# Head laid out anew with 20 quads of raw rows, and SyncE fetching the rows of every 54th quad by one DMA per edge

## The chip, the cores and the metric

One core of a Trainium2 chip runs the whole kernel. The metric is the device time of one execution, in microseconds (us). The engines are TensorE (PE, with its weight loads PEld), VectorE (DVE), ScalarE (ACT), GpSimd (POOL) and SyncE (SP); each works through its own queue of instructions in order and waits for the others by semaphores. DMAs are issued from SP, ACT and POOL and run beside the engines.

## The reference

A graph layer on 12500 nodes (64 scalars and 32 vectors of 3, D = 160 numbers each) and 400000 edges, which are sorted by destination. Cut to what matters:

```python
h_s = s @ lin1_ws * a / sqrt(64);  h_v = einsum('nci,cd->ndi', v, lin1_wv) * a / sqrt(32)
w = silu(edge_scalars @ fc_w1 / 8) @ fc_w2 / 8          # 224 weights for each edge, in five parts
es, ev = h_s[edge_src], h_v[edge_src]                   # a random row of 160 for each edge
m_s1 = w1 * es * e0;  m_v1 = w2 * es * e1;  m_v2 = w3 * ev * e0   # m_s2, m_v3: dot and cross products
agg = segment_sum(concat(m...), edge_dst)
out = layernorm(x + gated(sc(x) + agg @ lin2))
```

## The kernel before

**Edges.** 400000 edges are 3125 tiles of 128. Four tiles are a quad, and the main loop runs 784 steps of one quad (the last ones shorter). All engines' instructions are written out in the order of that loop (`manual_schedule`), so an engine's queue holds them as the code has them.

**Head.** Seven loads of nodes (`load`: xa, xz) are multiplied by lin1 and written as the table `h_tab` (12500 x 160) in DRAM. While the table is not there yet, GpSimd gathers rows of x itself ("raw rows") for 16 quads, every 30th from step 24 on, four gathers each (`gather_raw`), with indices loaded by `load_raw_columns` (raw_cols), and ACT writes them to `raw_tab`. Two raw quads follow each chunk of nodes, the rest the last chunk. `dt` (all destinations) is loaded by ACT at the end of the head; `rel`, the place of each edge in its window of 16 nodes, is made from it.

**A step.** `gather` issues four indirect DMAs on GpSimd (hg<-h_tab,idx, 128 rows of 640 B each; pool `deep`, four buffers). `weights` multiplies hid by w2 into PSUM (pw), `products` on VectorE multiplies pw by the gathered rows (pr), `select_quad` makes the one-hot matrix, and `add_tile` sums pr over a window of nodes (pa). Results are turned (pt), multiplied by lin2 (po, `second`) and added into acc; finished nodes leave through `finish`. In a raw quad the rows come back from `raw_tab` (rg), and six stages (`raw_stage`, one in each of the six steps before) turn them, multiply them by lin1 and find their factors, so that the step needs no gather.

**SyncE** issues the plain loads: idx and eat (indices and edge attributes, 15 steps at a time), es (edge scalars, two DMAs for 6 steps, two buffers), xs and xv (every 30 steps), rg, xt, and the stores of the output. Each DMA that is issued from SP or ACT signals one of eight semaphores in turn, and waits for the landing of the DMA that had the same one before.

Of the kernel before, what the change touches and what calls it, by code (L numbers as in the profile page):

```python
# [10 lines left out]
F32 = mybir.dt.float32  # L11
I32 = mybir.dt.int32
I16 = mybir.dt.int16
BF16 = mybir.dt.bfloat16
AF = mybir.ActivationFunctionType
OP = mybir.AluOpType
# [31 lines left out]
RAW_TILES = (0, 1, 3, 4)  # L48

CYC = [(i, (i + 1) % 3, (i + 2) % 3) for i in range(3)]  # L50
# [8 lines left out]
def gnn_kernel(  # L59
# [160 lines left out]

    def load_raw_columns(r):

        t = steps[RAW_STEPS[r]][2][0][0]
        assert [u for u, _, _ in steps[RAW_STEPS[r]][2]] == [t + k for k in RAW_TILES]
        k = 0
        while k < 5:
            g, u = divmod(t + k, GT)
            m = min(5 - k, GT - u)
            nc.sync.dma_start(raw_cols[:, r, k:k + m], src[g][:, u:u + m])
            k += m  # L230

# [12 lines left out]
    def load_bases():  # L244

        nc.sync.dma_start(row0, dst[0:1])
# [3 lines left out]
        nc.sync.dma_start(rows[:even], bounds[0, :even * NO].rearrange("(g k) -> g k", k=NO))  # L250
        if even < NG:
            nc.sync.dma_start(rows[even:, :NB - even * NO], bounds[:, even * NO:NB])
# [6 lines left out]
    with tc.tile_pool(name="nodes", bufs=len(starts)) as nodes, tc.tile_pool(  # L259
        name="nodes_ps", bufs=6, space=PSUM  # L260
    ) as nps, tc.tile_pool(name="z_ps", bufs=2, space=PSUM) as zps:
        loaded = []

        def load(c0):
# [15 lines left out]
        def load_maps():  # L280

            raw = ends_pool.tile([2 * S, NWT], F32, name="raw")
            for half in range(2):
                r = slice(half * S, (half + 1) * S)
                nc.sync.dma_start(w1[r, r], fc_w1)
                nc.sync.dma_start(raw[r], fc_w2)
            return raw
# [13 lines left out]

        load(starts[0])
        at = consts.tile([P, NT], F32, name="at")
        nc.scalar.dma_start(at, attr)
        ath = consts.tile([P, NT], F32, name="ath")
        nc.vector.tensor_scalar_mul(ath, at, 0.5)

        l1 = consts.tile([P, P], F32, name="l1")
        nc.vector.memset(l1, 0.0)
        nc.scalar.dma_start(l1[:S, :S], lin1_ws)  # L310
        for i in range(2):
            r = slice(S + i * V, S + (i + 1) * V)
            nc.scalar.dma_start(l1[r, r], lin1_wv)
        scales = [(l1[:S], 1.0 / math.sqrt(S)), (l1[S:], 1.0 / math.sqrt(V))]

        def scale():
            for m, by in scales:
                nc.vector.tensor_scalar_mul(m, m, by)
            scales.clear()

        def block_diagonal(name, w, n, scale, queue=nc.scalar):
            k = w.shape[0]
            m = consts.tile([n * k, n * k], F32, name=name)
            nc.vector.memset(m, 0.0)
            for i in range(n):
                queue.dma_start(m[i * k:(i + 1) * k, i * k:(i + 1) * k], w)
            if scale != 1.0:
                scales.append((m, scale))
            return m

        l1z = block_diagonal("l1z", lin1_wv, 4, 1.0 / math.sqrt(V))
        for m, by in scales:
            nc.scalar.mul(m, m, by)
        scales.clear()
        for i in range(3):
            nc.scalar.dma_start(l1v[i::3, i * V:(i + 1) * V], lin1_wv)
        scales.append((l1v, 1.0 / math.sqrt(V)))
        for r in range(4):
            load_raw_columns(r)
        for c0 in starts[1:3]:  # L340
            load(c0)
        for r in range(4, RAWS):
            load_raw_columns(r)
        load_bases()
# [10 lines left out]
        for k, c0 in enumerate(starts):  # L355
            if k + 3 < len(starts):
                load(starts[k + 3])
            elif k + 3 == len(starts):
                index(0)
            _, cn, quarters, cq, xa, xz = loaded[k]  # L360
            if c0 == 3 * CH:
                bases()
            ht = nodes.tile([P, 4 * U, D], F32, name="ht", bufs=3)
# [44 lines left out]
    raw = load_maps()  # L408
    load_chunk(0, nc.scalar)
    nc.scalar.dma_start(dt, dst)  # L410
    nc.vector.tensor_copy(iota_p, iota_i)
# [10 lines left out]
    nc.sync.dma_start(scs, sc_ws)  # L422
    scv = block_diagonal("scv", sc_wv, 3, 1.0 / math.sqrt(V), nc.sync)


# [11 lines left out]
    for to, part, pieces, w, r0, c0, by in maps:  # L437
        for k, piece in enumerate(pieces):
            four, at_p = divmod(PIECE[piece], 4)
            m = terms.setdefault((to, part, four), len(terms))  # L440
            at_r = at_p * V
            r = l2[at_r:at_r + V, m, c0:c0 + w.shape[1]]
            nc.sync.dma_start(r, w[r0 + k * V:r0 + (k + 1) * V])
            scales.append((r, by))
    assert len(terms) == 11
    scales.append((scs, 1.0 / math.sqrt(S)))

# [239 lines left out]
    with tc.tile_pool(  # L687
# [4 lines left out]
        name="deep", bufs=4  # L692
    ) as deep, tc.tile_pool(name="raw", bufs=1) as raw_pool, tc.tile_pool(name="pw_ps", bufs=2, space=PSUM) as pw_ps, tc.tile_pool(
        name="pa_ps", bufs=2, space=PSUM
# [24 lines left out]
        def fetch(n):  # L719
# [4 lines left out]
            if n + 6 < len(steps):  # L724
                c, i, _ = steps[n + 6]
                if i == 0:
                    load_chunk(c)

        turned_rows = {}
        attrs = {}  # L730

        def fetch_raw(n):

            if n + 8 in raw_of:
                T = n + 8
                rg = raw_pool.tile([P, Q, D], F32, name="rg", bufs=1)
                nc.sync.dma_start(rg.rearrange("p t d -> p (t d)"), raw_tab[raw_of[T]])
                attrs[T] = [rg]

        def raw_stage(T, k):  # L740
# [3 lines left out]
            def flat():  # L744
                return raw_pool.tile([P, Q * P], F32, name="flat", bufs=3)

# [43 lines left out]
            elif k in (2, 1):  # L790
                if k == 2:
                    turned_rows[T] = raw_pool.tile([P, Q, D], F32, name="hs", bufs=1)
                c = slice(0, S) if k == 2 else slice(S, D)
# [128 lines left out]
        with tc.manual_schedule(  # L922
# [9 lines left out]
            products_due = []  # L932
            checks = farthest(late)
            for n, (c, i, tiles) in enumerate(steps):
# [172 lines left out]
```

## Time and profile before

| | |
|---|---|
| median of 3 runs | 4002.86 us (4002.58 to 4004.17) |
| profiled execution | 4002.3 us, span 4000.5 us |
| TensorE busy | 3371.9 us (84%), granted clock 0.925 |
| VectorE busy | 2410.4 us (60%) |
| ScalarE busy | 1002.1 us (25%) |
| GpSimd busy | 2971.0 us (74%) |
| bytes moved | 422.84 MB, mean 106 GB/s |

Busy times are shares of the span. In a line of the groups stand line, engine, operation, out<-in and count, then busy time and mean ns of one, then the idle time of the engine before these instructions and what ended most of it. A line of the waits has the waiting engine and line, whom it waited for, and us in total, times and longest. In the order of time stand start, duration and instruction, with idle time before it in brackets; "x12" is a run of equal rows and its duration reaches from the first's start to the last's end. A line of windows has the length, then busy time of PE, PEld, DVE, ACT and POOL with counts, granted clock, busy share of the DMA engines and GB/s.

### The profile page before, as it was taken

How to read it: one execution, taken by the hardware profiler on the slowest of the kernel's cores; microseconds unless marked ns; L12 is line 12 of the kernel's file. 1: busy time of each engine (PE TensorE's matmuls, PEld its weight loads, DVE VectorE, ACT ScalarE, POOL GpSimd, SP SyncE). 2: the span in 40 equal slices, each digit the busy share in tenths (PEclk: the TensorE clock that was granted, in tenths of full speed). 3: DMA queues.
4: the chain of work that ended last, by engine and by line, in shares of the span. 5: the costliest groups of instructions: out<-in, count | busy, mean ns of one | idle time of the engine just before them, and what ended most of it. 6: DMA issues, size and time to landing. Idle time of an engine off the chain costs nothing. (4 is left out here: it accounts for less than half of the span.)

```text
span 4000.5 us, 55637 instructions
## 1 busy us (share of the span) xinstructions
PE 3371.9 (84%) x17991; PEld 1683.7 (42%) x17991; DVE 2410.4 (60%) x6505; ACT 1002.1 (25%) x3235; POOL 2971.0 (74%) x3133
## 2 busy tenths in 40 slices
PE   4598898898888889889899889788789888888887
PEld 4244444444444444444444444344344344344443
DVE  2465665666666666656666656556556565665655
ACT  0322222222222222223222222222122222221222
POOL 5677777777777777777777777777777777777775
PEclk7699999999999999999999999999899989999998
DMA  8634444434444443444444443444443443443442
GB/s 205 167 93 109 102 107 101 111 95 101 113 99 107 105 109 96 110 103 104 104 102 104 101 114 95 99 105 98 99 106 95 109 99 95 106 102 95 101 99 62
DMA packets 297291, 422.84 MB, mean 106 GB/s; under 512 B 76356, under 2 KB 241232, under 8 KB 296097
## 3 DMA queue, kind: packets, MB, share of 16 engines
q0 software_dynamic: 150000, 256.20, 24.9%
q1 hardware_dynamic: 130720, 147.26, 16.7%
q10 hardware_dynamic: 16274, 15.74, 1.3%
q8 instruction: 147, 2.41, 0.3%
q14 instruction: 150, 1.23, 0.1%
HBM read 397.71 MB, written 21.25 MB: 105 GB/s over the span
## 5 line engine op out<-in xcount | busy, mean ns | idle before, releaser
L490 POOL DMA_INDIRECT hg<-h_tab,idx x3061 | 2907.3, 950 | 946.9 <-issue 835.5
L578 PE MATMUL pa<-pr,sel 128*64 128x416 f32 x6250 | 1355.7, 557 | 1.4 <-DVE pw L557 1.4
L512 DVE TENSOR_TENSOR pr<-pw,hg 128x512 f32<-128x512 f32 x766 | 529.3, 691 | 1033.1 <-DMA hg<-h_tab,idx 1020.0
L502 PE MATMUL pw<-w,hid 64*128 64x224 f32 x6250 | 865.4, 392 | 338.3 <-DVE acc L611 227.0
L520 DVE TENSOR_TENSOR pr<-pw,hg 128x384 f32<-128x384 f32 x2298 | 1137.8, 547 | 0.0
L502 PEld LDWEIGHTS pw<-w,hid 64*128 64x128 f32 x6250 | 576.7, 195 | 635.6 <-issue 540.6
L578 PEld LDWEIGHTS pa<-pr,sel 128*64 128x64 f32 x6250 | 398.7, 143 | 576.5 <-issue 554.2
L850 ACT COPY sa<-pa 128x416 f32<-128x416 f32 x521 | 263.3, 505 | 1062.3 <-PE pa L578 1057.9
L481 PE MATMUL ph<-es,w 128*128 128x512 f32 (+1 forms) x784 | 455.5, 664 | 42.9 <-DMA es<-in_es_t_dram 29.8
L483 ACT ACTIVATE hid<-ph 128x512 f32<-128x512 f32 x392 | 233.6, 596 | 670.4 <-PE ph L481 670.0
L557 DVE TENSOR_TENSOR pw<-rel,iota_p 128x64 f32<-128x64 int16 x782 | 178.8, 229 | 339.6 <-PE pw L502 335.0
L587 PEld LDWEIGHTS pt<-ident,sa 128*128 128x128 f32 (+1 forms) x2084 | 223.8, 134 | 296.9 <-issue 231.1
L587 PE MATMUL pt<-ident,sa 128*128 128x128 f32 (+1 forms) x2084 | 337.0, 286 | 7.6 <-ACT hid L483 4.2
L603 PE MATMUL po<-tt,l 128*96 128x256 f32 (+3 forms) x1360 | 314.2, 378 | 13.8 <-DVE y L643 11.2
L571 DVE TENSOR_TENSOR sel<-pw,eas 128x256 f32<-128x256 f32 x766 | 317.2, 414 | 0.0
L591 ACT COPY tt<-pt 128x192 f32<-128x192 f32 x521 | 164.9, 316 | 487.8 <-PE pt L587 486.0
L603 PEld LDWEIGHTS po<-tt,l 128*96 128x96 f32 x1360 | 212.0, 164 | 124.5 <-issue 56.6
L481 PEld LDWEIGHTS ph<-es,w 128*128 128x128 f32 x784 | 121.8, 196 | 322.1 <-issue 230.8
L611 DVE TENSOR_TENSOR acc<-acc,os 96x32 f32 x1042 | 197.9, 190 | 24.0 <-ACT os L606 5.5
L637 PE MATMUL pp<-ident,acc 96*128 96x96 f32 x196 | 39.6, 288 | 94.4 <-DVE pw L557 45.8
L606 ACT COPY os<-po 96x512 f32<-96x512 f32 (+2 forms) x68 | 38.4, 564 | 317.4 <-PE po L603 301.9
L593 ACT COPY tt<-pt 128x32 f32<-128x32 f32 x521 | 102.2, 196 | 0.0
(105 smaller groups left out, 1123.6 us busy)
## 6 DMA issues: line engine op xcount, KB each, us to landing
es<-in_es_t_dram SPq DMA_DIRECT2D x258, 384.0 KB
hg<-h_tab,idx POOLq DMA_INDIRECT x3061
h_tab<-ht ACTq DMA_DIRECT2D x6, 1280.0 KB
xt<-in_x_dram SPq DMA_DIRECT2D x23, 320.0 KB
out_dram<-y SPq DMA_DIRECT2D x23, 320.0 KB
raw_tab<-raw_rows ACTq DMA_DIRECT2D x16, 320.0 KB
rg<-raw_tab SPq DMA_DIRECT2D x16, 320.0 KB
xv<-in_xv_t_dram SPq DMA_DIRECT2D x25, 187.5 KB
```

Source lines behind the costliest of these rows:

```text
L481: nc.tensor.matmul(ph[:k, c], w1[:k, :k], es[:k, t0 * P + c0 * P:t0 * P + c1 * P], start=True, stop=True)
L483: nc.scalar.activation(hid[:k, c], ph[:k, c], AF.Silu, scale=1.0 / math.sqrt(64))
L490: nc.gpsimd.indirect_dma_start(out=hg[:, t, :], out_offset=None, in_=h_tab, in_offset=bass.IndirectOffsetOnAxis(ap=i, axis=0))
L502: nc.tensor.matmul(pw[:, t, :NWT], hid[r, c * P:(c + 1) * P], w2[r], start=True, stop=True)
L512: nc.vector.tensor_mul(two, pw[:, :n, :2 * S].rearrange("p t (k c) -> p t k c", k=2), hg[:, :n, None, :S].to_broadcast([P, n, 2, S]))
L520: nc.vector.tensor_mul(pr[:, :n, first:first + V3].rearrange("p t (i c) -> p t i c", i=3), pw[:, :n, None, 2 * S + k * V:2 * S + (k + 1) * ...
L571: nc.vector.tensor_mul(sel[:, :n], oh[:, :, None, :].to_broadcast([P, n, 4, W]), e[:, :, :, None].to_broadcast([P, n, 4, W]))
L578: nc.tensor.matmul(pa[half * ROWS:(half + 1) * ROWS, :NPR], sel[:, t].rearrange("p k w -> p (k w)"), pr, start=start, stop=stop)
L587: nc.tensor.transpose(pt[:c, four * P:four * P + k], sa[:k, four * P:four * P + c], ident[:k, :k])
L603: nc.tensor.matmul(po[:, k, :nb], l2[:b, terms[to, part, four]], a[:, :nb], start=(n == 0), stop=(n == len(of) - 1))
L611: nc.vector.tensor_add(window, window, os[:, :, b])
L850: nc.scalar.copy(sa, pas.pop(j)[:, :NPR])
```

## The change

Three things are done. (1) The head has 20 raw quads instead of 16, three after each chunk of nodes; raw_cols comes in two DMAs ahead of everything else, all seven loads of nodes follow each other, and the first es and dt move from ACT's queue to SP's. The weights' diagonal blocks and the l2 matrix are loaded in fewer, wider DMAs and copied with a scale by VectorE. (2) Of 14 quads (steps 63, 117, ... 765) the rows are fetched by SyncE: four steps ahead of the start it loads the indices (cols), VectorE multiplies them by 640 and TensorE turns them, so that one partition holds 128 byte addresses (line). From step T - 51 on SyncE loads 32 of these at a time into registers and issues one DMA of 640 B for each edge, 512 for a quad, spread evenly over 49 steps. The one buffer hs takes the place of hg in step T. (3) Of the raw stages' buffers, flat has two instead of three, and rg and the result share one.

```diff
-RAWS = 16
+RAWS = 20
+OFF_FIRST = 63
+OFF_EVERY = 54
+OFF_LEAD = 51
+OFF_MARGIN = 2
+LOT = 32
 ...
+        load_raw_columns(0, 4)
+        nc.scalar.dma_start(l1[:S, :S], lin1_ws)
+        nc.scalar.dma_start(wv4, times(4, lin1_wv))
 ...
         load(starts[0])
+        load_raw_columns(4, RAWS)
+        for c0 in starts[1:]:
+            load(c0)
+        nc.sync.dma_start(row0, dst[0:1])
+        index(0)
+        raw = load_maps()
+        load_chunk(0)
+        nc.sync.dma_start(dt, dst)
 ...
-            rg = nodes.tile([P, Q, D], F32, name="raw_rows", bufs=8)
+            rg = nodes.tile([P, Q, D], F32, name="raw_rows", bufs=10)
 ...
-            for _ in range(2 if c0 < starts[-1] else len(raws)):
+            for _ in range(3 if c0 < starts[-1] else len(raws)):
                 gather_raw(raws.pop(0))
-    load_chunk(0, nc.scalar)
-    nc.scalar.dma_start(dt, dst)
 ...
+            def turn(self, cols):
+                nc.vector.tensor_scalar(at_byte, cols, float(ROW), None, op0=OP.mult)
+                nc.tensor.transpose(pl, at_byte, ident)
+                nc.vector.tensor_copy(line, pl)
 ...
+                def lot(k, p0):
+                    _, values = nc.values_load_multi_w_load_instructions(
+                        line[k:k + 1, p0:p0 + LOT], engines=[ENG.SP], min_val=0,
+                    for j, v in enumerate(values):
+                        nc.sync.dma_start(
+                            hs[p0 + j:p0 + j + 1, k].bitcast(U8),
+                            self.flat[ds(v, ROW)].rearrange("(o d) -> o d", o=1))
+                        yield
 ...
+                    if n == T - OFF_LEAD - 4:
+                        self.cols = self.begin(T)
+                    if n == T - OFF_LEAD - 1:
+                        self.line = self.turn(self.cols)
+                    if n == T - OFF_LEAD:
+                        self.todo.append((T, self.fetch(T, self.line), [0]))
 ...
+                    upto = min(Q * P, -(-Q * P * (n + 1 - T + OFF_LEAD) // of))
+                    while done[0] < upto:
+                        next(every)
+                        done[0] += 1
 ...
-                hg = (turned_rows.pop(n) if n in raw_of
+                off.step(n)
+                hg = (off.rows(n) if n in off.steps
+                      else turned_rows.pop(n) if n in raw_of
                       else gather(deep, [index(t) for t, _, _ in tiles]))
```

GpSimd's whole queue before, from the making of the identity on (raw_rows are gathers of x in the head, hg those of the main loop):

```order
masks.py:199 AFFINE_SELECT ident<-ident 128x128
L207 IOTA iota_i 128x128
L239 IOTA share 1x1042
L349 DMA raw_rows<-in_x_dram,raw_cols 128x160 x64
L490 DMA hg<-h_tab,idx 128x160 x3061
L1001 TENSOR_LOAD redo
```

and after:

```order
masks.py:199 AFFINE_SELECT ident<-ident 128x128
L216 IOTA iota_i 128x128
L248 IOTA share 1x1042
L351 DMA raw_rows<-in_x_dram,raw_cols 128x160 x80
L502 DMA hg<-h_tab,idx 128x160 x2989
L1098 TENSOR_LOAD redo
```

Sixteen gathers have moved into the head, and 56 are gone.

SyncE's queue before, at the first steps of the main loop:

```order
L159 DMA idx<-in_src_dram 128x60
L160 DMA eat<-in_ea_dram 128x240
L198 DMA es<-in_es_t_dram 64x4x384 x4
L824 DMA xs_1069<-in_xs_t_dram 64x500
L826 DMA xv_1071<-in_xv_t_dram 96x500
L737 DMA rg<-raw_tab 128x640
L159 DMA idx<-in_src_dram 128x5
L160 DMA eat<-in_ea_dram 128x20
```

and after, at the same place, where the first of the 14 quads begins:

```order
L168 DMA idx<-in_src_dram 128x60
L169 DMA eat<-in_ea_dram 128x240
L207 DMA es<-in_es_t_dram 64x4x384 x2
L760 DMA cols<-in_src_dram 128x2 x2
L207 DMA es<-in_es_t_dram 64x4x384 x2
L781 TENSOR_LOAD line
L786 DMA hs<-h_tab 1x640 x21
L917 DMA xs_1168<-in_xs_t_dram 64x500
L919 DMA xv_1170<-in_xv_t_dram 96x500
L786 DMA hs<-h_tab 1x640 x11
L781 TENSOR_LOAD line
L786 DMA hs<-h_tab 1x640 x10
```

Between the loads stand ten or eleven row DMAs for each step now, and every load is queued behind them.

ScalarE's queue before, at the end of the head (the last writes of the table, then what the main loop needs first):

```order
L400 DMA h_tab<-ht 128x160
L403 DMA h_tab<-ht 84x160
L352 DMA raw_tab<-raw_rows 128x640 x4
L198 DMA es<-in_es_t_dram 64x4x384 x2
L410 DMA dt<-in_dst_dram 128x3125
L483 ACT_TABLE_LOAD
```

and after:

```order
L399 DMA h_tab<-ht 128x160
L402 DMA h_tab<-ht 84x160
L354 DMA raw_tab<-raw_rows 128x640 x2
L408 DMA l1v<-in_lin_wv_dram 32x32 x3
L495 ACT_TABLE_LOAD
L495 ACTIVATE hid<-ph 128x512
```

es and dt have left it; they stand on SyncE behind the loads of nodes.

More of the change, by code (lines that the diff above doesn't have):

```diff
@@ L219, in gnn_kernel, with load_raw_columns @@
     nc.vector.memset(l1v, 0.0)
[L221 to L230, printed above, removed]
+    def load_raw_columns(a, b):
+        for r in range(a, b):
+            t = steps[RAW_STEPS[r]][2][0][0]
+            assert [u for u, _, _ in steps[RAW_STEPS[r]][2]] == [t + k for k in RAW_TILES]
+            assert divmod(t, GT) == (r, RAW_TILE0 - 5 * r) and t + 5 <= (r + 1) * GT
+        of = src[a][:, RAW_TILE0 - 5 * a:][:, :5]
+        nc.sync.dma_start(raw_cols[:, a:b],
+                          bass.AP(tensor=of.tensor, offset=of.offset,
+                                  ap=[of.ap[0], [P * GT - 5, b - a], [1, 5]]))
     w1 = consts.tile([2 * S, 2 * S], F32, name="w1")
@@ L262, in gnn_kernel, with times @@
         loaded = []
+        def times(n, w):
+            return bass.AP(tensor=w.tensor, offset=w.offset, ap=[[0, n], *w.ap])
         def load(c0):
@@ L285, in load_maps @@
                 nc.sync.dma_start(w1[r, r], fc_w1)
-                nc.sync.dma_start(raw[r], fc_w2)
+            nc.sync.dma_start(raw, times(2, fc_w2))
             return raw
@@ L305, in gnn_kernel @@
+        nc.scalar.dma_start(wv4, times(4, lin1_wv))
+        nc.vector.tensor_scalar_mul(l1[:S, :S], l1[:S, :S], 1.0 / math.sqrt(S))
+        for q in range(4):
+            r = slice(q * V, (q + 1) * V)
+            nc.vector.tensor_scalar_mul(l1z[r, r], wv4[r], 1.0 / math.sqrt(V))
+            if q >= 2:
+                nc.vector.tensor_scalar_mul(l1[r, r], wv4[r], 1.0 / math.sqrt(V))
         ath = consts.tile([P, NT], F32, name="ath")
         nc.vector.tensor_scalar_mul(ath, at, 0.5)
-        l1 = consts.tile([P, P], F32, name="l1")
@@ L309, in gnn_kernel @@
[L309 to L314, printed above, removed]
+        load(starts[0])
+        load_raw_columns(4, RAWS)
[5 more added lines that the diff above has]
+        load_chunk(0)
@@ L316, in scale @@
+        nc.sync.dma_start(dt, dst)
+        scales = []
         def scale():
-            for m, by in scales:
-                nc.vector.tensor_scalar_mul(m, m, by)
+            for m, of, by in scales:
+                nc.vector.tensor_scalar_mul(m, of, by)
             scales.clear()
[L321 to L344, printed above, removed]
@@ L355, in gnn_kernel @@
         for k, c0 in enumerate(starts):
[L356 to L359, printed above, removed]
             _, cn, quarters, cq, xa, xz = loaded[k]
             if c0 == 3 * CH:
+                load_bases()
                 bases()
@@ L403, in gnn_kernel @@
                 nc.scalar.dma_start(h_tab[c0 + full * P:c0 + cn, :], ht[:n, full])
-            for _ in range(2 if c0 < starts[-1] else len(raws)):
+            for _ in range(3 if c0 < starts[-1] else len(raws)):
                 gather_raw(raws.pop(0))
-    raw = load_maps()
-    load_chunk(0, nc.scalar)
-    nc.scalar.dma_start(dt, dst)
+    for i in range(3):
+        nc.scalar.dma_start(l1v[i::3, i * V:(i + 1) * V], lin1_wv)
+    scales.append((l1v, l1v, 1.0 / math.sqrt(V)))
     nc.vector.tensor_copy(iota_p, iota_i)
@@ L422, in gnn_kernel @@
     nc.sync.dma_start(scs, sc_ws)
-    scv = block_diagonal("scv", sc_wv, 3, 1.0 / math.sqrt(V), nc.sync)
+    scales.append((scs, scs, 1.0 / math.sqrt(S)))
+    scv = consts.tile([V3, V3], F32, name="scv")
+    nc.vector.memset(scv, 0.0)
+    wv3 = ends_pool.tile([V3, V], F32, name="wv3")
+    nc.sync.dma_start(wv3, bass.AP(tensor=sc_wv.tensor, offset=sc_wv.offset,
+                                   ap=[[0, 3], *sc_wv.ap]))
+    for i in range(3):
+        r = slice(i * V, (i + 1) * V)
+        scales.append((scv[r, r], wv3[r], 1.0 / math.sqrt(V)))
+    of_l2 = {}
+    for w, name in ((lin2_ws, "w2s"), (lin2_wv, "w2v")):
+        n = w.shape[0] // V
+        of_l2[name] = ends_pool.tile([P, n, w.shape[1]], F32, name=name)
+        for a in range(4):
+            nc.sync.dma_start(of_l2[name][a * V:(a + 1) * V],
+                              w.rearrange("(b r) c -> r b c", r=V))
     al_s = 0.25 / math.sqrt(96)
@@ L735, in fetch_raw @@
                 T = n + 8
[L736 removed]
+                rg = raw_pool.tile([P, Q, D], F32, name="rg", tag="rows", bufs=1)
                 nc.sync.dma_start(rg.rearrange("p t d -> p (t d)"), raw_tab[raw_of[T]])
@@ L933, in gnn_kernel @@
             checks = farthest(late)
+            off = Off()
+            assert not set(off.steps) & set(raw_of)
             for n, (c, i, tiles) in enumerate(steps):
```

65 lines of the change are left out of this document (57 added, 8 removed).

## The prediction

> **What bounds the kernel now.** I read the page's groups of instructions first, then the waits, then GpSimd's and VectorE's order of time at both ends.
>
> ```profile
> span 4000.5 us, 55637 instructions
> L490 POOL DMA_INDIRECT hg<-h_tab,idx x3061 | 2907.3, 950 | 946.9 <-issue 835.5
> DVE pr L512 <- DMA hg<-h_tab,idx: 1020.0, 431, 8.0
> POOL hg L490 <- DVE pr L520: 18.1, 44, 5.0
> 114.20 0.94 POOL L349 DMA_INDIRECT raw_rows<-in_x_dram,raw_cols  x1 [0.30 <-issue]
> 124.39 0.94 POOL L490 DMA_INDIRECT hg<-h_tab,idx  x1 [9.25 <-DMA l<-in_lin_wv_dram]
> 125.64 0.95 POOL L490 DMA_INDIRECT hg<-h_tab,idx  x1 [0.30 <-issue]
> 3968.39 0.94 POOL L490 DMA_INDIRECT hg<-h_tab,idx  x1 [0.30 <-DVE pw L557]
> ```
>
> GpSimd issues 3061 gathers between 124.39 and 3968.39 us: 3844.0 / 3060 = 1.256 us each, and the undisturbed pitch is 125.64 - 124.39 = 1.25. It is saturated: its own waits on VectorE are 18.1 us in all, while VectorE waits 1020 us for gathers. So the time is the head (124.4), 3061 pitches (3844), and 32.1 us from the last gather to the end of the span. The profiled execution took 4002.3 us against the median of 4002.86; I sum against 4002.3.
>
> TensorE is the next limit, and has room:
>
> ```profile
> 152.00:3970.00 3818.00, 3308.40 (x17639) 1631.48 (x17637) 2356.72 (x6356) 985.35 (x3194) 2889.77 (x3045) 0.94 0.42 102
> L786 PE MATMUL prt<-ident,rg 128*64 128x128 f32 (+1 forms) x128 | 19.9, 278 | 0.8 <-ACT hid L483 0.7
> ```
>
> The first number after the window's length is TensorE's busy time: 3308 / 784 steps = 4.22 us a step, VectorE's (third) 3.01. The granted clock is 0.94.
>
> **The change, part by part.**
>
> *Fewer gathers.* Four more raw quads and 14 quads for SyncE take 18 x 4 = 72 gathers out of the 3061: 72 x 1.256 = 90.4 us off GpSimd's steady part. The average step then has 2989 x 1.256 / 784 = 4.79 us. A raw quad issues 24 small matmuls, four quads 96 x 0.278 = 27 us on TensorE, and 14 transposes of offsets about 4 us: 4.26 us a step, 89% of 4.79. That lies beside the gathers, as long as the four buffers of hg even out the heavy steps. A skipped quad lets GpSimd run one step, 5 us, ahead; where a raw quad and a SyncE quad stand three steps apart (114 and 117, 171 and 174, 384 and 387) it may reach the end of its buffers. The longest such wait now is the 5.0 us above; I charge 8 us in all.
>
> *The head.* Sixteen more raw gathers stand in it, 16 x 1.25 = 20 us of GpSimd. Before, it starts them late and idles at the end:
>
> ```profile
> 14.18 1.10 POOL L349 DMA_INDIRECT raw_rows<-in_x_dram,raw_cols  x1 [11.73 <-DMA raw_cols<-in_src_dram]
> 17.36 23.61 SPq L229 DMA_DIRECT2D raw_cols<-in_src_dram  x12
> 0.00:50.00 50.00, 15.52 (x90) 15.06 (x91) 8.64 (x20) 2.21 (x4) 25.20 (x32) 0.73 0.63 130
> 50.00:100.00 50.00, 27.18 (x161) 25.01 (x160) 16.48 (x25) 1.15 (x3) 26.98 (x28) 0.75 0.98 280
> 100.00:150.00 50.00, 9.03 (x27) 4.26 (x25) 14.82 (x51) 6.11 (x11) 28.25 (x29) 0.53 0.77 227
> 123.81 0.77 ACTq L410 DMA_DIRECT2D dt<-in_dst_dram  x1
> 136.89 7.10 DVE L450 TENSOR_TENSOR rel<-dt,lo 128x520 int16<-128x520 int32 x6 [28.18 <-DMA dt<-in_dst_dram]
> 148.89 0.69 DVE L512 TENSOR_TENSOR pr<-pw,hg 128x512 f32<-128x512 f32 x1
> 151.25 0.94 POOL L490 DMA_INDIRECT hg<-h_tab,idx  x1 [5.03 <-DVE pr L520]
> ```
>
> Now the first index columns go out first on SyncE, so GpSimd starts near 5 us instead of 14.2, and 80 raw gathers end at 5 + 100 = 105 at the earliest. The other floor is the DMA engines: they move 280 GB/s when full (0.98 busy). Four more raw quads read and write 4 x 2 x 328 KB = 2.6 MB, and dt (1.6 MB) and the first es (0.8 MB) come ahead of the gathers instead of after: 5 MB more. By the windows 50 x 130 + 50 x 280 + 24.4 x 227 = 26 MB went before 124.4 us; 31 MB at 280 GB/s is 111 us, with a slow start 116. I take the first gather at 113 us (105 to 118): -11.4 us. dt now lands before the table is done, so rel stands off the path, the first product follows the first gather by some 6 us, and the 5.03 us wait at 151.25 goes: -5. What is late next there is the table itself, that is, the DMA engines.
>
> *SyncE's rows.* This decides. A quad is 512 DMAs of 640 B and 16 loads of 32 registers, all in SyncE's one queue, with a rotation of eight landing semaphores: each DMA waits for the one eight earlier. No DMA of one row at a register's address is in the trace; the nearest are those to or from one partition:
>
> ```profile
> 41.01 0.29 SPq L246 DMA_DIRECT2D row<-in_dst_dram  x1
> 45.33 0.30 SPq L250 DMA_DIRECT2D rows<-bounds  x1
> 45.68 0.25 SPq L252 DMA_DIRECT2D rows<-bounds  x1
> 45.98 0.49 SPq L270 DMA_DIRECT2D xa<-in_xs_t_dram  x1
> 2098.78 0.33 SPq L159 DMA_DIRECT2D idx<-in_src_dram  x1
> 2099.21 0.38 SPq L160 DMA_DIRECT2D eat<-in_ea_dram  x1
> 2099.69 35.49 SPq L198 DMA_DIRECT2D es<-in_es_t_dram  x4
> L875 DVEq TENSOR_LOAD <-rows x68: 543/1126/2425, 218.9 to 3980.5; - x68
> ```
>
> The pitch from one issue to the next is 45.98 - 45.68 = 0.30 for two elements of one partition, 0.35 (45.68 - 45.33) for 65 partitions, 0.43 (2099.21 - 2098.78) and 0.48 for 128. The far ends are 0.25 (the issue alone) and 23.61 / 12 = 1.97, where each issue waited behind the large loads. I take 0.30, the row nearest in shape: 512 x 0.30 = 154 us. A register load took 1.13 us for 16 values on VectorE and 0.54 at least, so some 0.04 a value, 1.8 us for 32: 16 x 1.8 = 29 us.
>
> [...]
>
> SyncE's other work and its present idleness come from its waits between 152 and 3970 us:
>
> ```profile
> SPq L198 <- PE pt L587: 1670.5, 83, 34.6
> SPq L159 <- DMA hg<-h_tab,idx: 883.5, 111, 28.9
> SPq L198 <- PE prt L786: 403.6, 14, 33.4
> SPq L675 <- DVE pw L557: 287.8, 20, 27.6
> SPq L198 <- PE ph L481: 209.9, 9, 32.9
> 122.31 1.39 ACTq L198 DMA_DIRECT2D es<-in_es_t_dram  x2
> 131.11 2.04 PE L481 MATMUL ph<-es,w 128*128 128x512 f32 x2 [29.79 <-DMA es<-in_es_t_dram]
> ```
>
> These five are 3455 of 3818 us, so its own loads take at most 363 / 14 = 26 us per 54 steps; I take 22, leaving the rest to waits too short to be listed here. New is that a row behind an es pair waits for its landing through the rotation: the pair landed 131.11 - 122.31 = 8.8 us after issue when the engines were full, and 3.1 us of that pass in issuing the pair and six rows. At 42% busy I take 6 us, a stall of 3, nine times in 54 steps, and 10 us for the other loads: 37 us (0 to 61). A quad is then 154 + 29 + 22 + 37 = 242 us.
>
> It may begin when VectorE has turned the columns at step T - 52, and must end by step T: 51.5 x 4.79 = 247 us. The next begins at T + 2, so the cycle is 242 + 3 steps = 256 us against 54 x 4.79 = 259. It fits, by 3 us. Once it doesn't, VectorE waits at step T, GpSimd fills its four buffers and stops, and every microsecond over costs 13 times itself.
>
> **Sum:** -90.4 - 11.4 - 5 + 8 = -98.8; 4002.3 - 98.8 = 3903.5 us, taken as 3904.
>
> **The rivals.**
>
> 1. *SyncE a little late.* Pitch 0.31 to 0.32, or 5 to 10 us more of stalls: cycle 260 to 266, 13 x (1 to 7) = 13 to 91 us given back: 3917 to 3995.
> 2. *SyncE is the bound: slower.* With a pitch of 0.35, as for 65 partitions, or a register's address costing 0.05 more: a quad 268, a cycle 280. SyncE's first quad begins at step 12, near 119 + 12 x 4.2 = 170 us; 170 + 268 + 13 x 280 + 19 x 4.79 + 31 = 4200 us. The point from which it decides: with a first quad of 255, (4000.5 - 170 - 255 - 122) / 13 = 266 us of cycle, a pitch of 0.32 (122 is the 19 steps and 31 us behind step 765). For it: the margin is 0.02 us an issue. Against it: the issue of two elements took 0.30 with its gap, and what a register's address adds no row shows.
> 3. *Each row costs what a load of 128 partitions does.* Pitch 0.43: a quad 308, a cycle 322: 170 + 308 + 13 x 322 + 122 = 4786 us. Against it: the single-partition rows are 0.25 to 0.30. [...]
> 4. *TensorE can't follow* a step of 4.79: half of the 90 us comes back, about 3950. Against it: 1020 us of VectorE waiting on gathers.
>
> **Chances.** Forecast 0.60 (3885 to 3925, from a first gather at 105 or 118 and 0 to 15 us of buffer waits). Rival 1 0.14, of which 0.05 lies within 0.2% (8 us, about what a measurement here can tell from none) and 0.01 beyond. Rival 2 0.14, rival 3 0.08, rival 4 0.04. So faster 0.60 + 0.08 + 0.04 = 0.72, same 0.05, slower 0.23. The range 3885 to 4100 leaves out most of rivals 2 and 3.
>
> **What would show it.** First gather near 113 us, first product some 6 us later; last gather 32 us before the end; a row's pitch on SyncE near 0.30 and SyncE still waiting for the turned offsets (line) or es buffers between quads. Wrong: VectorE waiting on DMAs of hs, with GpSimd waiting on VectorE just before; then the pitch or the stalls behind es were mis-sized. A gather's pitch above 1.26 would mean that 7168 small packets disturb the gathers.

## The result, and the profile after

The changed kernel takes 3930.36 us (median of 4 runs, 3926.78 to 3934.17) against 4002.84 for the kernel before, measured beside it: a ratio of 0.9821 with a 95% interval of 0.9806 to 0.9835. The forecast was 3904. The profiled execution took 3931.9 us for a span of 3929.8, 70.7 us shorter than the span before. The kernels below ran on several chips: on three of them, called slow chips here, the kernel before took 5196 to 5298 us at a granted clock near 0.83, on the others 4000 to 4003 us at 0.92 to 0.93, and each kernel is compared with before on its own chip.

GpSimd first: the page's groups, the waits, and GpSimd's order of time (start, length, engine, line) at the two ends of its gathers.

```profile
span 3929.8 us, 70593 instructions
L502 POOL DMA_INDIRECT hg<-h_tab,idx x2989 | 2837.5, 949 | 927.6 <-issue 800.8
DVE pr L524 <- DMA hg<-h_tab,idx: 836.4, 386, 5.7
POOL hg L502 <- DVE pr L532: 30.0, 77, 3.3
3.38 1.10 POOL L351 DMA_INDIRECT raw_rows<-in_x_dram,raw_cols  x1 [0.93 <-DMA raw_cols<-in_src_dram]
117.92 7.71 POOL L351 DMA_INDIRECT raw_rows<-in_x_dram,raw_cols  x1 [17.65 <-DMA raw_tab<-raw_rows]
128.44 0.95 POOL L351 DMA_INDIRECT raw_rows<-in_x_dram,raw_cols  x1 [0.30 <-issue]
139.28 0.94 POOL L502 DMA_INDIRECT hg<-h_tab,idx  x1 [9.90 <-DMA l1v<-in_lin_wv_dram]
3893.46 0.95 POOL L502 DMA_INDIRECT hg<-h_tab,idx  x1 [0.30 <-issue]
```

GpSimd still sets the pace: 2988 pitches between 139.28 and 3893.46 are 3754.2 us, 1.2564 us each against 1.2562 before, and VectorE still waits 836 us for gathers. The sum of the difference in span is then short:

| part | before | after | difference |
|---|---|---|---|
| 72 gathers fewer at 1.256 | | | -90.4 |
| first gather of the table | 124.39 | 139.28 | +14.9 |
| pitch over 2988 gathers | 1.2562 | 1.2564 | +0.6 |
| last gather to the end | 32.1 | 36.3 | +4.2 |
| all | 4000.5 | 3929.8 | -70.7 |

The gathers gave what they should; the head, which was to give 11.4 us, took 14.9. GpSimd itself stood in it: its last four raw gathers waited 17.65 us for a buffer that a write of raw rows still held, and ended at 129.4 us, not at 105. The first product follows the first gather by 6.7 us (145.99), where some 6 had been forecast.

Now SyncE: the tile view of the rows that it fetches (x count, nanoseconds min/median/max of one, first and last start in us), the same for its register loads, its waits, and a stretch of its order of time round one quad.

```profile
L786 SPq DMA_DIRECT2D hs<-h_tab x7168: 217/228/403, 202.0 to 3802.2; - x200
L786 SPq MOVE hs<-h_tab x7168: 29/29/38, 201.5 to 3802.2; - x200
  DVE pw L569: 0.8, 5
L781 SPq TENSOR_LOAD <-line x224: 1880/2130/2361, 199.0 to 3784.7; - x112
SPq L781 <- DVE pw L569: 164.1, 14, 16.2
SPq L786 <- DMA es<-in_es_t_dram: 152.4, 136, 2.5
1218.76 6.01 SPq L786 DMA_DIRECT2D hs<-h_tab  x10
1231.66 1.28 SPq L207 DMA_DIRECT2D es<-in_es_t_dram  x2
1240.97 23.08 SPq L786 DMA_DIRECT2D hs<-h_tab  x63
1469.49 6.24 SPq L786 DMA_DIRECT2D hs<-h_tab  x10
```

One quad runs from 1240.97 to 1475.7, 235 us. From the first row of the first quad to the last of the fourteenth are 3600.2 us; with a median of 237 us for a quad (by the issue times of all rows) the cycle is (3600.2 - 237) / 13 = 258.7 us, which is 54 steps of 4.79. The third row says whether it was enough: before the products that read hs, VectorE was idle 0.8 us behind its own work, and never for a DMA. SyncE instead waited for VectorE, at its first register load of each quad (164.1 us, 14 times).

### The profile page after: what moved, and what is told of

Same layout as the page of the kernel before. It is cut to its first block, busy times and chain, and to the rows that moved or that the text cites. A ratio compares the mean times of both kernels' runs of the same rounds, so it can differ in the third digit from the quotient of the medians.

```text
span 3929.8 us, 70593 instructions
## 1 busy us (share of the span) xinstructions
PE 3360.2 (86%) x18149; PEld 1685.3 (43%) x18149; DVE 2427.2 (62%) x6562; ACT 1011.0 (26%) x3252; POOL 2922.2 (74%) x3077
## 5 line engine op out<-in xcount | busy, mean ns | idle before, releaser
L502 POOL DMA_INDIRECT hg<-h_tab,idx x2989 | 2837.5, 949 | 927.6 <-issue 800.8
L590 PE MATMUL pa<-pr,sel 128*64 128x416 f32 x6250 | 1338.3, 551 | 1.4 <-DVE pw L569 1.4
L532 DVE TENSOR_TENSOR pr<-pw,hg 128x384 f32<-128x384 f32 x2244 | 1110.1, 547 | 0.0
L514 PE MATMUL pw<-w,hid 64*128 64x224 f32 x6250 | 847.6, 386 | 251.6 <-DVE acc L623 186.4
L524 DVE TENSOR_TENSOR pr<-pw,hg 128x512 f32<-128x512 f32 x748 | 516.9, 691 | 851.1 <-DMA hg<-h_tab,idx 836.4
L514 PEld LDWEIGHTS pw<-w,hid 64*128 64x128 f32 x6250 | 564.2, 192 | 543.3 <-issue 440.0
L351 POOL DMA_INDIRECT raw_rows<-in_x_dram,raw_cols x80 | 82.9, 1036 | 44.0 <-issue 22.2
```

Of the source, the lines that this page charges most:

```text
L502: nc.gpsimd.indirect_dma_start(out=hg[:, t, :], out_offset=None, in_=h_tab, in_offset=bass.IndirectOffsetOnAxis(ap=i, axis=0))
L514: nc.tensor.matmul(pw[:, t, :NWT], hid[r, c * P:(c + 1) * P], w2[r], start=True, stop=True)
L524: nc.vector.tensor_mul(two, pw[:, :n, :2 * S].rearrange("p t (k c) -> p t k c", k=2), hg[:, :n, None, :S].to_broadcast([P, n, 2, S]))
L532: nc.vector.tensor_mul(pr[:, :n, first:first + V3].rearrange("p t (i c) -> p t i c", i=3), pw[:, :n, None, 2 * S + k * V:2 * S + (k + 1) * ...
L590: nc.tensor.matmul(pa[half * ROWS:(half + 1) * ROWS, :NPR], sel[:, t].rearrange("p k w -> p (k w)"), pr, start=start, stop=stop)
```

## The experiments

Theory A of the study: the changed head is late, because its transfers stand one behind the other in two queues with one rotation of semaphores; the rest goes as forecast. Its rival, theory B: the head is bound by bytes. Beside that stands the question whether SyncE's rows have the narrow margin that the prediction gave them.

### The parts of the change, each alone

*e6_off_only*: the head of before with its 16 raw quads, and the 14 quads of SyncE. (It ran under the name e2_off_only on a slow chip as well, and the row-early kernel below as e1_row0_early; those are told at the end.)

```diff
+OFF_FIRST = 63
+OFF_EVERY = 54
+OFF_LEAD = 51
 ...
+            off = Off()
 ...
-                hg = (turned_rows.pop(n) if n in raw_of
+                off.step(n)
+                hg = (off.rows(n) if n in off.steps
```

(In part, and against the kernel before; the smaller buffers of the raw stages come along.)

> Head and 16 raw quads as before, the 14 quads on SyncE taken over, once more for a chip on which the gathers set the pace: 56 x 1.256 = 70 us less than before, 3932 us (3928 to 3940), first gather near 124 us, the gathers' pitch 1.256, no wait of VectorE for hs. Then the new head and the four more raw quads together bring nothing. If SyncE's rows disturb the gathers: pitch over 1.26, time over 3950.

3940.67 us, ratio 0.9848 [0.9832, 0.9865], 0.7 us above the range that was expected.

```profile
123.70 0.95 POOL L498 DMA_INDIRECT hg<-h_tab,idx  x1 [9.68 <-DMA l<-in_lin_wv_dram]
```

First gather 123.70, 3005 gathers at 1.2580, 36.1 us behind the last: 56 x 1.256 = 70.3 less for gathers, 5.4 more for the pitch, 4.0 more for the end. So SyncE's quads alone bring 61.7 us of span, and the new head with its four more raw quads, added to them, the other 9.0 of the change: not nothing, as the expectation had it.

*e9_no_off*: the new head with its 20 raw quads, no quad for SyncE.

```diff
-                self.steps = list(range(OFF_FIRST, len(steps) - 12, OFF_EVERY))
+                self.steps = []
```

> The changed kernel without any SyncE quad (their list of steps is empty; the head with 20 raw quads stays): 3045 gathers. Theory A (the time is first gather + gathers x 1.2564 + about 32 to 36, and the head of the change gives the first gather at 139 instead of 124): 139 + 3044 x 1.2564 + 32 = 3996 and 2 us around the span, 3998: within 0.3% of before, so 16 gathers fewer bought nothing. Theory B (the head itself gives the 20 us of its 16 gathers, and it is the SyncE quads that delay the start): first gather near 124, time about 3982.

3986.94 us, ratio 0.9967 [0.9955, 0.9978].

```profile
135.48 0.94 POOL L502 DMA_INDIRECT hg<-h_tab,idx  x1 [9.20 <-DMA l1v<-in_lin_wv_dram]
POOL hg L502 <- DVE pr L532: 10.7, 35, 0.3
```

It has theory A's late start (135.48, 11 us behind before), but a better time than its 3998. The pitch is 1.2539, 0.0023 x 3044 = 7.0 us less than before: the wait of 5.03 us at 151.25 is gone, as the prediction said, and little else waits: the 10.7 us of waits for VectorE's products are 35 ordinary pauses of 0.30. So 16 gathers fewer (-20.1), the head (+11.1), the pitch (-7.0) and the rest (+0.3) are -15.7, against the measured -15.9 of span. With SyncE's quads the pitch goes back to 1.2564, 0.0025 x 2988 = 7.5 us: those are the waits for buffers that were charged at 8. The waits show them: 30.0 us in 77 in the change are 77 pauses of 0.30 and 6.9 us more. The smaller buffers of the raw stages are in this kernel too, and cost nothing that its sum shows.

### SyncE's margin

*e8_every48*: a quad every 48 steps instead of 54, all else as changed.

```diff
-OFF_EVERY = 54
-OFF_LEAD = 51
+OFF_EVERY = 48
+OFF_LEAD = 45
```

> The changed kernel with a SyncE quad every 48 steps (lead 45) instead of 54 (51): 16 quads instead of 14, so 8 gathers, 10 us of GpSimd, fewer; SyncE needs about 237 us a quad and some 13 to 18 between two, 250 to 255, against 48 x 4.8 = 230 us of a cycle. Theory A (SyncE's own issue sets a hard limit just under the spacing of 54 steps): SyncE binds, each cycle is about 250 us instead of 230, VectorE waits for hs or for what stands on SyncE behind the rows, and the time is 4150 to 4300. Theory B (the rows are not near a limit, the cycle that was seen was only paced by the gathers): 3918 to 3930.

4234.3 us, ratio 1.0583 [1.0561, 1.0604]. It makes 15 quads, not the 16 that I had counted. The tile view of hs, the group of the first product that reads it, and VectorE's wait:

```profile
L786 SPq DMA_DIRECT2D hs<-h_tab x7680: 217/227/399, 229.2 to 3982.0; - x197
  DVE pr L524: 210.5, 14
L524 DVE TENSOR_TENSOR pr<-pw,hs 128x512 f32<-128x512 f32 x15 | 10.4, 692 | 223.4 <-DMA hs<-h_tab 210.5
L493 PE MATMUL ph<-es,w 128*128 128x512 f32 (+1 forms) x784 | 503.9, 728 | 496.6 <-DMA es<-in_es_t_dram 486.5
```

Now SyncE binds. A row costs what it cost before (227 ns). The cycle is (3982.0 - 229.2 - 240) / 14 = 250.9 us, where 48 steps would be 229.9: 14 x 21.0 = 294 us lost, against 304 between the medians of this kernel and of the change. VectorE waits 210 us for hs, and TensorE 487 us for es, which stands in the same queue behind the rows. So SyncE needs 250.9 us from quad to quad here; the change allows 258.7. The margin is 8 us in 259, and six steps closer costs the whole gain four times over.

### The head

The windows of the head in before and in the changed kernel, in four stretches up to the first gather of the table (the columns are busy time and count of PE, PEld, DVE, ACT and POOL; the last three are the granted clock, the busy share of the DMA engines, and GB/s):

```profile
0.00:30.00 30.00, 10.27 (x56) 9.81 (x56) 1.90 (x9) 2.21 (x4) 12.38 (x19) 0.84 0.74 144
30.00:70.00 40.00, 16.26 (x102) 14.91 (x102) 15.99 (x24) 0.00 (x0) 27.96 (x29) 0.67 0.77 208
70.00:100.00 30.00, 16.16 (x91) 15.36 (x92) 7.23 (x11) 1.15 (x3) 11.84 (x13) 0.73 0.91 261
100.00:124.40 24.40, 1.32 (x7) 0.89 (x5) 2.02 (x13) 0.00 (x0) 11.50 (x14) 0.50 0.88 278
```

```profile
0.00:30.00 30.00, 10.16 (x73) 9.97 (x73) 9.40 (x25) 0.00 (x0) 20.89 (x28) 1.00 0.95 173
30.00:70.00 40.00, 9.28 (x48) 8.63 (x48) 4.15 (x6) 0.71 (x1) 30.25 (x32) 0.59 0.99 281
70.00:100.00 30.00, 5.41 (x13) 3.31 (x14) 4.05 (x5) 1.82 (x4) 22.77 (x24) 0.50 0.77 189
100.00:139.30 39.30, 15.65 (x125) 14.59 (x124) 19.41 (x41) 0.72 (x1) 10.84 (x6) 0.72 0.90 284
```

The whole head, up to the first gather of the table, as rows of before, the change, e5 and e7 (told below), and the bytes moved in the first two:

```profile
0.00:124.40 124.40, 44.02 (x254) 40.97 (x254) 27.14 (x57) 3.36 (x7) 63.68 (x73) 0.69 0.82 219
0.00:139.30 139.30, 40.49 (x256) 36.49 (x256) 37.01 (x77) 3.25 (x5) 84.75 (x89) 0.69 0.91 238
0.00:132.40 132.40, 48.30 (x256) 43.22 (x256) 36.76 (x75) 3.02 (x5) 78.70 (x88) 0.72 0.93 246
0.00:130.50 130.50, 45.99 (x256) 41.49 (x256) 36.87 (x75) 3.12 (x5) 78.42 (x88) 0.70 0.92 250
```

```profile
DMA packets 24856, 27.26 MB, mean 219 GB/s; under 512 B 6248, under 2 KB 20241, under 8 KB 24082
DMA packets 27788, 33.22 MB, mean 238 GB/s; under 512 B 6929, under 2 KB 22277, under 8 KB 26886
```

The change has 6.0 MB more to move before its first gather. Two of its stretches are slow. In the first 30 us the DMA engines are 0.95 busy and still move only 173 GB/s. Between 70 and 100 there is a hole, 0.77 busy and 189 GB/s, in which TensorE and VectorE stand idle. This is what stood in it (order of time of SyncE, VectorE and TensorE, and SyncE's wait):

```profile
85.19 0.31 SPq L336 DMA_DIRECT2D row<-in_dst_dram  x1
92.89 0.83 DVE L255 COPY bases_row<-row 1x1042 int32<-1x1042 int32 x1 [49.35 <-DMA row<-in_dst_dram]
94.59 3.99 PE L308 MATMUL hp<-base_f,ones 1*128 1x512 f32 x6 [51.79 <-DVE base_f L304]
SPq L283 <- DMA h_tab<-ht: 43.1, 3, 16.5
```

The row of destinations, 12 KB, is queued on SyncE behind the loads of all seven chunks of nodes; those wait in the rotation of semaphores for writes of the table, 43.1 us in three waits; and the copy of that row, and the matmuls on it, stand on VectorE and TensorE ahead of the fourth chunk. A load issued at 85.19 (at 41.01 before) therefore holds four of seven chunks until 98.6.

*e5_row0_early*: this one load moved forward.

```diff
         load(starts[0])
+        nc.sync.dma_start(row0, dst[0:1])
         load_raw_columns(4, RAWS)
         for c0 in starts[1:]:
             load(c0)
-        nc.sync.dma_start(row0, dst[0:1])
```

> The kernel with row loaded behind the first chunk's loads once more, for a chip on which TensorE's granted clock is near 0.93 and the gathers set the pace, as in the two profiles compared. Theory A (VectorE, TensorE and ScalarE stand still for row from 42.8 to 92.9 us, and that delays the table): VectorE's wait for row falls under 10 us and the first gather comes at 118 to 130 us instead of 139.3, the time at 3908 to 3922 us. Rival B (the DMA engines or the rotation of semaphores set the head): the wait goes, the first gather stays at 135 to 140, the time within 4 us of 3930.

3923.71 us, ratio 0.9802 [0.9785, 0.9818]. VectorE no longer waits for the row, and the hole is full:

```profile
0.00:30.00 30.00, 10.90 (x73) 10.71 (x73) 9.20 (x25) 0.00 (x0) 21.82 (x29) 1.00 0.93 173
70.00:100.00 30.00, 15.75 (x88) 15.35 (x88) 8.06 (x17) 2.44 (x4) 22.67 (x24) 0.72 0.94 269
```

But the first gather came only 6.9 us earlier, at 132.42, outside what theory A had given and outside rival B's 135 to 140 as well; so was the time. The size of this gain is less sure than one trace makes it: the head of the changed kernel, line for line the same, gave its first gather at 139.28 in the change, 137.04 in e8 and 135.48 in e9, so the row is worth 3 to 7 us, and the intervals of the two ratios overlap. So the hole was one cause, and not the whole. GpSimd's wait for a buffer has gone with it: the raw gathers end at 107.3 us here, and GpSimd then waits 25.2 us for the first gather of the table.

*e7_raw_writes_later*: in addition the writes of raw rows issued on ScalarE's queue one chunk later, behind the next write of the table.

```diff
-            nc.scalar.dma_start(raw_tab[r], rg.rearrange("p t d -> p (t d)"))
+            held.append((r, rg))
 ...
+            write_raw(len(held))
             for _ in range(3 if c0 < starts[-1] else len(raws)):
                 gather_raw(raws.pop(0))
+        write_raw(len(held))
```

> The changed kernel with the row of destinations loaded early (as in e5_row0_early) and, beside it, each chunk's three writes of raw rows issued on ScalarE's queue behind the next chunk's write of the table, not ahead of it. Theory A (what the first gather still waits for in e5 is ScalarE's queue, in which the table's writes stand behind writes of raw rows that wait for their gathers and for the rotation of semaphores): the table's last write goes out near 105 us instead of 123.18, the first gather of the table at 110 to 120 instead of 132.42 (not ahead of the last raw gather, 106.33 in e5), and the time falls by the same 12 to 22 us, to 3902 to 3912. Theory B (the first 120 us are bound by the bytes of all DMAs, so their order on one queue only moves the wait): the first gather stays at 128 to 134, time 3920 to 3926.

3920.61 us, ratio 0.9798 [0.9781, 0.9814], first gather at 130.52. Its interval overlaps e5's; it is the fastest kernel of the study by the median. Theory B's numbers came true, but this run doesn't show its cause. These are the last writes on ScalarE's queue and the first gather behind them, in the change and then in e7:

```profile
132.61 0.86 ACTq L402 DMA_DIRECT2D h_tab<-ht  x1
133.66 1.03 ACTq L354 DMA_DIRECT2D raw_tab<-raw_rows  x2
118.15 0.56 ACTq L408 DMA_DIRECT2D h_tab<-ht  x1
121.94 4.71 ACTq L358 DMA_DIRECT2D raw_tab<-raw_rows  x5
130.52 0.95 POOL L510 DMA_INDIRECT hg<-h_tab,idx  x1 [16.19 <-DMA l1v<-in_lin_wv_dram]
```

The first gather follows the issue of the last raw rows by 3.9 us in e7 and 4.6 in the change, but that of the table's last write by 11.8 and 5.8. The semaphores in the traces say why: ahead of its first gather GpSimd's queue waits in turn for all eight semaphores of the loads and writes (from 134.3 to 138.6 us in the change), so for the writes of raw rows too. In the change the table had landed at 136.9 us and the last raw rows at 138.5, and the gather started 0.8 us later; in e7 the table had landed by 125.1, the raw rows at 129.7, and again the gather started 0.8 us later. (The view puts both waits down to l1v, whose loads use the same semaphores.) The raw rows lie in the pool of the head (`nodes`), which ends where the buffers of the main loop begin; that this is why the gather has to wait for them no run shows by itself. So e7 put later what the first gather waits for, and what the table's writes alone would have given it can't tell.

Up to the first gather the DMA engines' busy time is 0.82 x 124.4 = 102 us in before, 0.91 x 139.3 = 127 in the change, 0.93 x 132.4 = 123 in e5 and 0.92 x 130.5 = 120 in e7. So the change raised the busy time by 25 us, which speaks for the bytes; but e5 and e7, which move the same rows in another order, took 4 to 7 us of it back, so busy time isn't a floor that the order leaves alone. How much of the late start is bytes and how much order stays open.

### The runs on slow chips

*e12_quarter_writes* was to test theory B by itself: as many transfers, in the same order, with fewer bytes.

```diff
-            nc.scalar.dma_start(raw_tab[r], rg.rearrange("p t d -> p (t d)"))
+            nc.scalar.dma_start(raw_tab[r][:, :D], rg[:, 0, :])
 ...
-                nc.sync.dma_start(rg.rearrange("p t d -> p (t d)"), raw_tab[raw_of[T]])
+                nc.sync.dma_start(rg, raw_tab[raw_of[T]][:, None, :D].to_broadcast([P, Q, D]))
```

> The changed kernel, in which each of the 20 writes of raw rows carries a quarter of its bytes (the first of the quad's four tiles, which is later read four times over; the other three tiles' rows are left out of the output). The number of transfers, their order, their queues and their waits are the same; 4.9 MB of the head's 33 MB are gone. Theory B (the start is bound by the bytes of all transfers, 239 GB/s over the first 139 us): the first gather comes 4.9 MB / 0.239 = 20 us earlier, 119 instead of 139.3, and the time is 20 us less, about 3911. Theory A (the start is a chain of waits between SyncE's and ScalarE's queues, which the size of the transfers only lengthens): the first gather stays at 131 to 140, time 3923 to 3932. Should the chip be the one on which before takes 5200 to 5300 us, the first gather stands against 157 there: 137 by B, over 149 by A.

5557.89 us, where before takes 5297.63 (1.0495 [1.0457, 1.0534]). First gather at 161.78, against 157 for this head on such chips (157.3 in e11 and 157.1 in e3, on two other slow chips): 4.9 MB fewer and no gain, as theory A says. There the engines are not full:

```profile
30.00:70.00 40.00, 7.49 (x20) 5.91 (x21) 2.03 (x3) 0.00 (x0) 28.88 (x31) 0.50 0.56 139
SPq L287 <- DMA h_tab<-ht: 50.9, 1, 50.9
```

One wait of SyncE for a write of the table, through the rotation, lasts 50.9 us there. So on that chip fewer bytes didn't help; it doesn't tell what they would bring where the engines are 0.91 busy. That stays untested.

*e10_raw_writes_last*: the row early, and 18 of the 20 writes of raw rows behind the whole table, with two buffers fewer for the nodes.

```diff
-            rg = nodes.tile([P, Q, D], F32, name="raw_rows", bufs=10)
+            rg = nodes.tile([P, Q, D], F32, name="raw_rows", bufs=RAWS - 2)
 ...
+            if c0 in starts[:2]:
+                load(starts[-2 + c0 // CH])
 ...
+        write_raw(len(held))
```

> The changed kernel with the row of destinations early, and 18 of the 20 writes of raw rows (5.9 MB) issued on ScalarE only behind the last write of the table and the loads of l1v; for their 18 buffers the node loads have 5 instead of 7, so the last two chunks are loaded as the first two are done. Theory B of the last run (the first gather waits for bytes: 33 MB at about 240 GB/s, a share of 0.91 of the DMA engines over the first 139 us of the changed kernel): 5.9 MB fewer ahead of the table are 20 to 24 us, the first gather of the table comes at 108 to 118 instead of 130.5 (the raw gathers alone end near 106), and the time is 3899 to 3910. Theory A (something other than the bytes, the chain of loads, chunks and writes with its rotation of semaphores, holds the table): the first gather stays at 126 to 134, time 3917 to 3926. If the writes that are now late hold a buffer that a first gather of the table needs, the first gather is early and the second or third quad waits for it, and up to 20 us come back.

5475.45 us against 5196.22 (1.0564 [1.049, 1.0639]). The first gather is later, not earlier:

```profile
173.30 0.94 POOL L513 DMA_INDIRECT hg<-h_tab,idx  x1 [50.42 <-issue]
146.43 21.20 ACTq L354 DMA_DIRECT2D raw_tab<-raw_rows  x18
SPq L287 <- DMA raw_tab<-raw_rows: 33.9, 1, 33.9
```

Two things meet: a load of nodes on SyncE waits 33.9 us, through the rotation, for a write of raw rows that stands on ScalarE; and GpSimd's first gather starts only as the 18 late writes end. The view names no releaser for the second, but it fits the wait that the semaphores of the change and of e7 show: the last raw rows went out at 167.6, and the gather came 5.7 us later, with the table long written. The expectation had allowed for buffers only of the second or third quad. Neither theory is decided by it.

*e11_no_last_quad* was to explain the 4 us longer end.

```diff
-                self.steps = list(range(OFF_FIRST, len(steps) - 12, OFF_EVERY))
+                self.steps = list(range(OFF_FIRST, len(steps) - 12, OFF_EVERY))[:-1]
```

> The changed kernel without the last of its 14 SyncE quads (step 765, 17 steps before the end of 782): 4 gathers more, 2993. Theory A (the last quad comes too near the end: GpSimd is done 5.0 us earlier, but VectorE and TensorE, which need 4.26 us of a step's 4.79, cannot draw its steps in before the end, which is why the stretch behind the last gather is 36.3 us instead of 32.1): the stretch behind the last gather goes back to 32 to 33, the last gather comes 5.0 later, and the time is the same within 2 us, 3929 to 3932. Theory B (the longer stretch has another cause, such as the store of the last results on SyncE): the stretch stays at 36 and the time is 5 us longer, 3934 to 3937.

5442.38 us against 5196.22 (1.0477 [1.0404, 1.0549]); 44.2 us behind the last gather, where the other kernels on such chips have 43.2 to 51.1. Nothing follows from that. That the quads lengthen the end is seen (36.1 to 36.8 us in every kernel with them on the usual chips, 32.1 and 32.4 without). That the last quad does it is unlikely: in e8 the last quad is step 735, 47 steps before the end instead of 17, and the end is still 36.2 us. The cause stays open.

*e1_row0_early, e2_off_only, e3_no_off and e4_every48* are e5, e6, e9 and e8 on a slow chip, where before took 5278.97 us.

> One line moved: the DMA of the first row of destinations (row) is issued right behind the first chunk's loads instead of behind all seven. Theory A (the head is late because VectorE, TensorE and ScalarE stand still from 42.8 to 92.9 us until row has landed): VectorE's wait for row falls from 49.4 us to under 10, the fourth to seventh chunks are multiplied as they land, the first gather comes near 122 us (118 to 130) instead of 139.3, and the time near 3914 us (3908 to 3922). Rival B (the DMA engines set the head: some 33 MB go before the first gather): the wait goes, but the first gather stays at 135 to 140, and the time within 4 us of 3930. Rival C (the loads of nodes wait for the landings of the table's writes in the shared rotation of eight semaphores): the same as B, with SyncE's waits for h_tab still above 40 us.

> Head and 16 raw quads as before; only the 14 quads on SyncE and the smaller raw buffers are taken over. If the steady part is GpSimd's gathers alone: 56 x 1.256 = 70 us less than before, 4002.8 - 70 = 3932 us (3928 to 3940), first gather at 124 us, no wait of VectorE for hs: then the new head and four more raw quads together bring nothing (20 us of gathers saved, 15 to 20 us of head lost). If SyncE's rows disturbed the gathers, the gathers' pitch would be above 1.26 and the time above 3950.

> The changed kernel with no quad on SyncE (its list of steps is empty), so 56 gathers more: 3930 + 70 = 4000 us (3996 to 4006) if SyncE's quads cost nothing else; below 3996 if they hold up something in the changed kernel, above 4006 if they spare more than their gathers. The first gather stays at 139 us, the gathers' pitch at 1.256.

> Every 48th quad and a lead of 45 steps: 15 quads instead of 14, a cycle of 48 x 4.78 = 229 us for SyncE's 237 us and 2 to 3 steps. If SyncE's length of a quad is a hard limit (my rival 2, brought about by a shorter cycle): the cycle is 237 + 12 = 249 us, 202 + 237 + 14 x 249 + 48 x 4.8 + 36 = about 4190 us (4100 to 4200), VectorE waits for hs at the 15 steps, GpSimd for VectorE. If SyncE has more room than I think (es waits hidden): 3930 - 4 x 1.256 = 3925 us.

They took 5534.45 (1.0495 [1.0453, 1.0537]), 5553.73 (1.0523 [1.0473, 1.0572]), 5301.79 (1.0057 [1.0034, 1.0081]) and, in one run, 5888.15 us. None of the four fits its numbers. GpSimd's largest wait in e3_no_off, and the tile view of hs in e1_row0_early:

```profile
POOL hg L502 <- DVE pr L532: 1355.4, 300, 10.8
L786 SPq DMA_DIRECT2D hs<-h_tab x7168: 1/225/1590, 244.4 to 5395.3; - x200
  DMA hs<-h_tab: 106.4, 12
```

In e3 GpSimd waits 1355 us for VectorE's products, so the gathers don't set the pace there, and 16 of them fewer bring nothing. In e1 the median row still issues in 225 ns, but single ones take up to 1.59 us, and the pitch from row to row (0.33 in the middle, against 0.32 on the other chips) is 1.44 us or more in a tenth of them. A quad takes 344 to 370 us instead of 237, the cycle becomes 369 (5395.3 - 244.4 - 356, over 13), and VectorE waits 106 us for hs. So on such a chip the kernels with SyncE's quads are some 5% slower than before. VectorE's waits for hs, the second rival's sign, are there, but they are less than half of the 233 us between e1 and e3; where the rest goes isn't settled, nor why these chips are slow. The changed kernel itself wasn't run on one of them.

## Why the prediction was right, and where its size was off

The gain has the cause that was named: GpSimd's gathers set the pace, and each one fewer gives a pitch. But 3930 lies outside the forecast's own 3885 to 3925 and inside the 3917 to 3995 of rival 1, whose cause did not occur: SyncE was in time, and the head was late. That the time still lies in the stated range is owed to its upper end of 4100, which was set for SyncE's sake, and for the head that is luck.

*Fewer gathers*, 72 x 1.256 = 90.4 us: right, since the pitch stayed.

*The wait at 151.25 and the buffers*, -5 and +8: right to 2 or 3 us; +0.6 was measured for both. The head without SyncE's quads shows 7.0 us less in the pitch, the quads put 7.5 back.

*The head*, -11.4 in the forecast and +14.9 measured (12.7 and 11.1 in the traces of e8 and e9), is the term that failed. By the spans the sum is 28.1 us short (-98.8 against -70.7): 26.3 from the head and 4.2 from the end, less 2.4 from the pitch. The head was worked out as a floor of bytes, 31 MB at 280 GB/s with 5 us for a slow start. Three things were off. The bytes were 33.2 MB, 119 us at 280: the 26 MB of before were 27.26 by its own window up to 124.4, and 6.0 were added, not 5. The first 30 us ran at 173 GB/s with the engines 0.95 busy, which is 30 x (280 - 173) / 280 = 11.5 us lost, not 5; the 280 came from before's window of 50 to 100 us, while its own first 30 us moved 144 GB/s at 0.74 busy. And the hole from 70 to 100 us at 189 GB/s lost 30 x 91 / 280 = 9.8 us. 118.6 + 11.5 + 9.8 = 139.9, against 139.28; this counts where the time went and doesn't show that bytes alone bound it. The first two are a matter of size. The third is a step that the prediction left out: it named the table as what is late next, but not that the row's load moves behind all nodes on SyncE while its copy stands ahead of the fourth chunk on VectorE. e5 undid that part and got 3 to 7 us. Two waits were put at nothing without a reason: that of the raw gathers for their ten buffers, 17.65 us, so that they ended at 129.4 instead of 105; and that of the first gather for the last raw rows, which landed 1.6 us behind the table in the change and at least 4.6 in e7. The prediction had named the table itself as what is late.

*SyncE's quad*, 242 us in the forecast, was 237, with its parts off in both directions: 512 rows at a pitch of 0.32 are 164 us (forecast 154 at 0.30); the 16 register loads of 32 values at 2.13 are 34 (29); what is left for other loads and stalls is 237 - 164 - 34 = 39 (59). Of that the waits behind es are 152.4 / 14 = 10.9 us, where 27 were charged: a wait lasted 152.4 / 136 = 1.1 us, not 3. The forecast of a cycle of 256 in 259 became 250.9 in 258.7, and e8 shows that a shorter spacing is paid in full.

*The end*, 32 us in the forecast, was 36.3: not foreseen, and not explained.

*The rivals.* The first and the second didn't occur in the change, but their mechanism is real: with less room (e8) SyncE binds, and the loss is 14 times what each cycle is over. The second's deciding point, a pitch of 0.32 with stalls of 37 us, was reached by the pitch but not by the sum, as the other loads and stalls were 20 us shorter. (Its cycle at a pitch of 0.35 is 268 + 14 = 282 us, not 280, which makes its 4200 some 30 us more.) The third fell: a row costs 0.32 from issue to issue, not 0.43. A row's issue takes 0.228 us and the move of its address 0.029. The fourth fell as well; VectorE kept waiting for gathers, 836 us.

## What to carry to other kernels

A queue that is to take over work is sized by its cycle, all that stands in it counted, against the cycle that it may take: here 251 of 259 us, and the gain holds; at 230 the kernel is 5.8% slower than before. When a head is laid out anew, follow the smallest load that the in-order engines need, and count bytes by the rate of their own stretch: full DMA engines (0.95 and 0.99 busy) moved 173 GB/s in one stretch and 281 in the next. A gather that seems to wait for its table may wait for everything that the head left under way, here for raw rows that landed 1.6 us behind the table: look at all the semaphores of its queue. A margin of 3% is also a bet on the chip: on the three slow ones a quad took 331 us or more, and the kernels with SyncE's quads were slower than before.

## What the hardware showed that I had not expected

- A row of 640 B at an address in a register: 0.228 us to issue on SyncE, 0.029 for the address's move, 0.32 from row to row, at the median of the 7168 rows of the change; 0.227 and 0.029 for issue and move in the 7680 of e8.
- A register load of 32 values takes 2.13 us (1.88 to 2.36) on SyncE; with the 1.13 us that 16 values took on VectorE before, about 0.07 us a value.
- DMA engines 0.95 busy moved only 173 GB/s in the loads and gathers of the first 30 us (0.74 busy and 144 GB/s in before, much the same rate for a busy engine), and 281 GB/s at 0.99 busy from 30 to 70 us, with writes of the table and of raw rows among them; that the mix makes the difference isn't shown.
- One rotation of semaphores ties SyncE's and ScalarE's queues: a load on SyncE stood 16.5 us (the change) and 50.9 us (e12) behind a write on ScalarE's queue.
- Chips differ: the kernel before took 4000 to 4003 us on some and 5196 to 5298 on three others, with the clock at 0.83; single row issues took up to 1.59 us there (e1), 0.40 in the change.
